# Two attention layers on one core: where the layer values, the last turn and the first weighted block stand in a hand-written order

## The chip, the cores and the metric

The kernel runs on one core of one Trainium2 chip. The metric is the device time of one execution in microseconds (us), the median over several executions. The hardware profiler records one execution more, with every instruction; durations in this text come from that record. Engines are named as in the profile: PE is TensorE (matrix products and turns), PEld its weight loads, DVE is VectorE, ACT is ScalarE, POOL is GpSimd, and SP is the engine that issues the transfers (DMA).

## The reference

The inputs are `x` (16 batches, 1024 nodes, 256 features, f32) and `adj` (16 x 1024 x 1024, int32, symmetric with ones on the diagonal). Every batch goes through two layers, each with a residual:

```python
# layer 0
h = relu(layernorm(x))
n = layernorm(h) * gamma1 + beta1                 # 8 heads of 32: q = k = v = n
a = softmax(where(adj > 0, n_q @ n_k.T / sqrt(32), -inf))
h = h + a @ n_k                                   # per head
x = x + h + gelu((layernorm(h) * gamma2 + beta2) @ W1 + b1) @ W2 + b2
# layer 1
f = relu(layernorm(x))
p = f @ W
l = (p @ a_1).T + p @ a_2 + (p @ a_12) @ p.T
t = softmax(where(adj > 0, leaky_relu(l, 0.2), -9e15))
x = x + elu(f @ W_1 + (t @ f) @ W_2)
```

The MLP is 256 to 1024 to 256. In the kernel the weights of layer 1 are folded beforehand: one matrix `wm` stands for `W a_12 W^T` in the logits, and `wo2` holds `W_2` with a further column `W a_1`, so that `gw = f @ wo2` gives the layer values `f @ W_2` and the term of `a_1` at once, and `(t @ f) @ W_2` becomes `t @ gw`.

## The kernel before, in words

**Two lanes of work.** All instructions of an engine run in the order in which the program lists them, and this order is planned by hand. The work is written as Python generators ("streams") that hand over after every piece, and each piece carries a place on a common scale; the stream with the smallest place goes on next. Two streams matter here. The attention of layer 0 for batch b+1 (`attention`) comes in units. The rest of batch b (`rest`: MLP, then layer 1) comes in pieces of 1.75 us planned width, or 0.9 for the short ones, and lies between those units. A piece that yields `True` moves the lane's place on. So one batch takes one repeat of about 210 us, and there are fourteen repeats with everything in them. The fifteenth MLP has no next prologue beside it, and the sixteenth has no attention beside it.

**Due times.** A planned clock advances with each piece and unit. `defer(t, f)` issues `f` when the clock has gone on by `t`; `run_deferred` issues what is due. So mask conversions, statistics, exponentials and transfers come into the order some pieces after the piece that asks for them. Other work waits as a turn: `ask(turn, c)` puts a turn of chunk `c` into a list, which `make_turns` works off between units; `wait_for(turn, c)` holds the lane until that has been done.

**The attention.** A batch has 8 key tiles of 128 and two halves of 512 queries. A unit computes the scores of four heads for one key tile (`s`, L994), VectorE adds the mask (L1007), ScalarE takes the exponential with its sums (L1014), and the product with the values follows a unit later (`o`, L1109). Because scores and mask are symmetric, one quarter of the exponentials isn't computed: while the first query half runs, `mirror` transposes blocks on VectorE (L1030), SP stores them to DRAM (`blocks`, L1037), and GpSimd adds them up (`part`, L1043) for the row sums, which SP stores as `rows` (L1058). For the second half `fetch(k)` loads them back as `em` (L1077), sixteen loads k = 0 to 15 per batch, eight for each of two head groups, and `weigh_mirrored(k)` multiplies them (`o`, L1091). `weigh_mirrored(k)` also defers `fetch(k + 2)` by 0.6: there are two buffers, so a load is issued only when the product two before it has used its buffer. In the second half a unit is followed by two such products. Three planned widths, which depend on the key tile, say how far the lane's place moves ahead of the first, between the two, and behind the second; what the other lane does in between follows from these (L1186):

```python
widths = ((0.8, 0.3, 0.05), (0.5, 0.45, 0.2), (0.4, 0.45, 0.3), (0.3, 0.5, 0.35))[kt - TPH]
yield widths[0]
weigh_mirrored(k)
yield widths[1]
weigh_mirrored(k + 1)
k += 2
yield widths[2]
```

SP also loads the int32 mask tiles (`adj`, L587), in halves that VectorE converts (L594); SP takes its instructions in order too.

**The rest of a batch.** Its 1024 rows are four chunks of two tiles. `expand(c)` is the first MLP product with its GELU (`ph`, `hid`), `contract(c, ..)` the second: per tile two pieces of four products into `po`, and then VectorE adds the residual into `xb` (L1327). `prepare1(c)` takes the statistics of a chunk and defers its normalized rows `ft` (L750, VectorE) by 5.0. `turn1(c)` transposes them on TensorE (`ptf`, L1349), and ScalarE writes them with a ReLU as `fT` (L1352). From `fT` come three things. `project_half(qh, oc)` gives `uT`, one output half `oc` for the query half `qh`, that is for two chunks (`puT`, L1364, copied by ScalarE, L1369). `values(t)` gives the layer values `gw` of one tile (`pg`, copied by VectorE for odd and by ScalarE for even tiles, L1379). `weights(c, i)` gives the logits of two key tiles `uT` for the queries of chunk `c` (`lg`); VectorE adds `gw`'s last column and the mask (L1397) and applies the leaky slope (L1402), ScalarE the exponential (L1403). Then `attend(t)` forms `own` (`pf`) and the product `pa` with the values, and stores the tile.

`ps_tile` gives every short product its PSUM tile from one pool of **three slots** (`ptf`, `po`, `puT`, `pg`, `lg`, `pa` and the turns of the next batch's prologue, `ptk`, among them): a product waits until the third product ahead of it has been read out. `with_values(pieces, c)` puts `values` of chunk `c` behind every second piece of a contraction, once `turn1(c)` has been made.

**The order around the change** is: `contract(2)` with the values of chunk 0 (tiles 0, 1), `contract(3)` with those of chunk 1 (tiles 2, 3), projection (0, 0), the last turn `turn1(3)`, projection (0, 1), values 4, logits 0, values 5, logits 1, projection (1, 0), values 6, projection (1, 1), values 7; then the remaining logits and `attend`.

Of the kernel before, what the change touches and what calls it, by code (L numbers as in the profile page):

```python
# [495 lines left out]
def fast_path(  # L496
# [29 lines left out]
    B, N, D = x.shape  # L526
# [9 lines left out]
    TPH = QW // P  # L536
# [25 lines left out]
    def ps_tile(shape, name, dtype=F32):  # L562
        return psm.tile(shape, dtype, tag="ps", name=name)
# [195 lines left out]
    def defer(us, f):  # L759
        deferred.append((clock[0] + us, len(deferred), f))  # L760

        return clock[0] + us
# [177 lines left out]
    def make_turns():  # L940
        room = 3 - open_sums[0] if open_sums[0] else 100
        while turns and turns[0][0] <= room:
            n, f = turns.pop(0)
            room -= n
            f()
# [22 lines left out]
    def attention(b, st):  # L968
# [96 lines left out]
        def gather(g):  # L1065
            r = blocks["sums", g] = denp.tile([P, NT // 2 * GH, TPH * GH], F32, tag="sums", bufs=1, name=f"gather_{b}_{g}")
            for a in range(GH):
                nc.sync.dma_start(
                    r[a * HD : (a + 1) * HD],
                    blocks["rows", g].rearrange("k (a i) e -> i (k a) e", i=HD)[:, :, a * TPH * GH : (a + 1) * TPH * GH],  # L1070
                )

        def fetch(k):
            g, t, half = k // (2 * TPH), k // 2 % TPH, k % 2
            if k == 0:
                blocks["e"] = midp.tile([P, 2, 2 * GH, P], F32, tag="mid0", name=f"em_{b}")
            nc.sync.dma_start(  # L1077
                blocks["e"][:, half],
                blocks[g][half * 2 * GH : (half + 1) * 2 * GH, t * GH : (t + 1) * GH].rearrange(
                    "k b i e -> (b i) k e"  # L1080
                ),
            )

        def weigh_mirrored(k):
            g, t, half = k // (2 * TPH), k // 2 % TPH, k % 2
            e = blocks["e"][:, half]
            if t == half == 0:
                acc[g, 1] = pso.tile([P, QW], F32, tag="o", name=f"o_{b}_{g}_1")
            o = acc[g, 1]
            for j in range(GH):  # L1090
                nc.tensor.matmul(  # L1091
                    o[j * HD : (j + 1) * HD, half * CW : (half + 1) * CW],
                    va[:, t, (g * GH + j) * HD : (g * GH + j + 1) * HD],
                    e[:, :, j * HD : (j + 1) * HD],
                    start=t == half == 0,
                    stop=False,
                )
            clock[0] += 0.45
            if k + 2 < 2 * TPH * NG:
                defer(0.6, lambda: fetch(k + 2))  # L1100
# [21 lines left out]
        def close(qh, g):  # L1122
            turns.append((1, lambda: finish(b, qh, g, *rl[g, qh], os[g, qh])))

        def invert(qh, g):
            r = smallp.tile([P, TPH, GH], F32, tag="rl", name=f"rl_{b}_{g}_{qh}")

            def f():
                if mirrored and qh == 0:
                    nc.vector.tensor_reduce(  # L1130
                        sums[0, g][:, :, :, 1].rearrange("p h t -> p t h"),
                        blocks["sums", g].rearrange("p k (t h) -> p t h k", h=GH),
                        axis=mybir.AxisListType.X,
                        op=ALU.add,
                    )
                nc.vector.tensor_reduce(
                    r.rearrange("p t j -> p j t"), sums[qh, g], axis=mybir.AxisListType.X, op=ALU.add
                )
                nc.vector.reciprocal(r, r)

            rl[g, qh] = r, defer(2.5 if mirrored and qh == 0 else 2.5, f)
# [8 lines left out]
        for n, u in enumerate(units):  # L1150
            qh, g, kt = u
            make_turns()
            es, rest_of_weights = scores(*u)
            go_on()
            rest_of_weights()
            first = n == 0 or units[n - 1][:2] != u[:2]
            last = n == len(units) - 1 or units[n + 1][:2] != u[:2]
            scored.append((weigh, (*u, es, first, last)))
            if not mirrored:
                if qh == NQH - 1 and kt % TPH == TPH - 1:  # L1160
                    invert(kt // TPH, g)
                    if kt < NT - 1:
                        close(kt // TPH, g)
                yield 1.0
                continue
            if qh == 0:
                if kt >= TPH:
                    mirror(g, kt, es)
                if n == NG * NT - 1:
                    defer(2.0, lambda: fetch(0))  # L1170
                    defer(2.2, lambda: fetch(1))
                if n == NT + 1:
                    gather(0)
                if n == NT + 3:
                    invert(0, 0)
                    close(0, 0)
                yield 1.0
                continue
            if n == NG * NT + 1:
                gather(1)  # L1180
            if n == NG * NT + 3:
                invert(0, 1)
                close(0, 1)
            if last:
                invert(1, g)
            widths = ((0.8, 0.3, 0.05), (0.5, 0.45, 0.2), (0.4, 0.45, 0.3), (0.3, 0.5, 0.35))[kt - TPH]  # L1186
            yield widths[0]
            weigh_mirrored(k)
            yield widths[1]
# [4 lines that stand above are left out]
    def go_on():  # L1194
        if scored:
            f, args = scored.pop()
            f(*args)
        clock[0] += 2.0
# [33 lines left out]
    def rest(b, st, tails):  # L1232
# [18 lines left out]
        def ask(turn, c):  # L1251

            def f():
                clock[0] += 0.5
                turn(c)
                turned.add((turn, c))
            turns.append((1, f))
            if not quarters[0]:
                make_turns()
# [49 lines left out]
        def contract(c, hid):  # L1309
            hid, ready = hid  # L1310
            run_deferred(ready)
            for i in range(TPC):
                t = c * TPC + i
                po = ps_tile([P, D], f"po_{b}_{t}")
                for f in range(FC):
                    matmul(
                        po,
                        hid[:, f, i * P : (i + 1) * P],
                        w2[:, f, :],
                        start=(f == 0),  # L1320
                        stop=(f == FC - 1),
                    )
                    if f == FC // 2 - 1:
                        open_sums[0] = 1
                        yield 1.75, True
                        open_sums[0] = 0
                nc.vector.tensor_add(xt[t], po, xt[t])  # L1327
                yield 1.75, True
# [128 lines left out]
        def with_values(pieces, c):  # L1457
            for i, piece in enumerate(pieces):
                yield piece
                if i % 2 == 1:  # L1460
                    yield from wait_for(turn1, c)
                    values(c * TPC + i // 2, st["fT"])
                    yield 0.9, i // 2 == 1
# [5 lines left out]
        hid = {0: (yield from expand(0))}  # L1469
# [16 lines left out]
        prepare1(1)  # L1486
        fT = st["fT"] = midp.tile([P, DC, N], F32, tag="mid1", name=f"fT_{b}")
        ask(turn1, 0)
        yield from with_values(contract(2, hid[2]), 0)
        prepare1(2)  # L1490
        ask(turn1, 1)
        yield from with_values(contract(3, hid[3]), 1)
        uT = midp.tile([P, DC, N], F32, tag="mid2", name=f"uT_{b}")
        prepare1(3)
        ask(turn1, 2)
# [1 line left out]
        def some_values(*ts):  # L1497
            for t in ts:
                values(t, fT)
                yield 0.9, t % 2 == 1  # L1500
# [5 lines left out]
        def some_weights(c, *pairs):  # L1506
            for i in pairs:
                first.append(weights(c, i))
                yield 1.75, True
# [2 lines left out]
        yield from wait_for(turn1, 0)  # L1512
        yield from wait_for(turn1, 1)
        yield from project_half(0, 0)
        if b < B - 1:
            ask(turn1, 3)
        yield from project_half(0, 1)
        if b == B - 1:
            ask(turn1, 3)
        yield from wait_for(turn1, 2)  # L1520
        yield from some_values(4)
        yield from some_weights(0, 0)
        yield from some_values(5)
        yield from some_weights(0, 1)
        yield from wait_for(turn1, 3)
        yield from project_half(1, 0)
        yield from some_values(6)
        yield from project_half(1, 1)
        yield from some_values(7)

        before = None
        for c in range(NCH):
# [186 lines left out]
```

## Time and profile before

| what | value |
|---|---|
| median of 3 runs | 3445.18 us (3441.09 to 3447.68) |
| the profiled execution | 3447.03 us |
| its span, first to last instruction | 3445.2 us |
| busy PE / DVE / ACT / POOL | 3250.0 / 2669.7 / 1987.4 / 1856.5 us |
| mean granted TensorE clock | 0.988 of full speed |
| moved by DMA | 404.81 MB, mean 118 GB/s |

The profiled execution stands 1.85 us above the median, and 1.8 us of it lie around the span. Busy times are sums over an engine's instructions; where a line of the profile names a releaser ("<- DVE ft"), it says what ended the idle time before the instruction. In a timeline each line holds start, duration, engine, source line, operation, result and operands, with the wait in brackets. PE's share of 94% says that it is almost never idle; where it is idle or slow in a repeat, and what is late there, has to be read from the timeline of a repeat.

### The profile page before, as it was taken

How to read it: one execution, taken by the hardware profiler on the slowest of the kernel's cores; microseconds unless marked ns; L12 is line 12 of the kernel's file. 1: busy time of each engine (PE TensorE's matmuls, PEld its weight loads, DVE VectorE, ACT ScalarE, POOL GpSimd, SP SyncE). 2: the span in 40 equal slices, each digit the busy share in tenths (PEclk: the TensorE clock that was granted, in tenths of full speed). 3: DMA queues.
4: the chain of work that ended last, by engine and by line, in shares of the span. 5: the costliest groups of instructions: out<-in, count | busy, mean ns of one | idle time of the engine just before them, and what ended most of it. 6: DMA issues, size and time to landing. Idle time of an engine off the chain costs nothing. (4 is left out here: it accounts for less than half of the span.)

```text
span 3445.2 us, 114688 instructions
## 1 busy us (share of the span) xinstructions
PE 3250.0 (94%) x48866; PEld 1597.5 (46%) x48866; DVE 2669.7 (77%) x4889; ACT 1987.4 (58%) x4808; POOL 1856.5 (54%) x2006
## 2 busy tenths in 40 slices
PE   6899999999999999999999999999999999999998
PEld 2244444444444444444444444444444444444477
DVE  5678787887878778787887887878788787877744
ACT  6765755647456474655646556575564745646542
POOL 4664663645656465563656737466364565635230
PEclk9999999999999999999999999999999999999999
DMA  5255455464554544545454555545546455554510
GB/s 134 50 123 145 104 122 125 112 159 102 128 120 116 144 112 122 129 114 143 112 133 112 122 139 119 140 106 125 125 112 159 100 131 118 121 142 102 128 38 14
DMA packets 741159, 404.81 MB, mean 118 GB/s; under 512 B 173217, under 2 KB 699937, under 8 KB 740641
## 3 DMA queue, kind: packets, MB, share of 16 engines
q1 hardware_dynamic: 740352, 397.14, 47.7%
q8 instruction: 386, 6.32, 0.8%
q14 instruction: 133, 1.08, 0.1%
q10 hardware_dynamic: 288, 0.26, 0.0%
HBM read 233.97 MB, written 146.54 MB: 110 GB/s over the span
## 5 line engine op out<-in xcount | busy, mean ns | idle before, releaser
L1014 ACT ACTIVATE e<-e 128x512 f32<-128x512 f32 x1504 | 929.3, 619 | 829.5 <-DVE e L1007 827.4
L1007 DVE TENSOR_TENSOR e<-s,mk 128x1024 f32<-128x1024 f32 x752 | 885.9, 1218 | 219.2 <-PE s L994 212.4
L574 PE MATMUL ph<-yT,w 128*32 128x256 f32 x7808 | 445.7, 379 | 23.5 <-DVE yT L1279 15.9
L574 PE MATMUL lg<-fT,uT 128*32 128x256 f32 x7680 | 455.7, 381 | 0.0
L994 PE MATMUL s<-kT 32*64 32x512 f32 x6272 | 451.3, 627 | 1.2 <-DVE e L1007 1.2
L574 PE MATMUL pa<-gw,e 128*32 128x258 f32 x7584 | 446.4, 380 | 0.1
L574 PE MATMUL po<-w,hid 128*32 128x256 f32 x7680 | 442.6, 379 | 0.0
L1109 PE MATMUL o<-e,va 128*32 128x512 f32 x3136 | 432.8, 619 | 1.4 <-ACT e L1014 1.4
L574 PEld LDWEIGHTS ph<-yT,w 128*32 128x32 f32 x7808 | 250.6, 110 | 226.8 <-DVE yT L1279 32.3
L574 PEld LDWEIGHTS po<-w,hid 128*32 128x32 f32 x7680 | 249.9, 110 | 203.0 <-issue 48.8
L574 PEld LDWEIGHTS lg<-fT,uT 128*32 128x32 f32 x7680 | 249.2, 110 | 195.3 <-issue 22.5
L574 PEld LDWEIGHTS pa<-gw,e 128*32 128x32 f32 x7584 | 247.5, 110 | 185.3 <-issue 26.2
L966 POOL TENSOR_TENSOR h<-h,ot 128x512 f32<-128x512 f32 x64 | 84.4, 1319 | 455.7 <-DVE ot L962 455.7
L1030 DVE STREAM_TRANSPOSE x<-e 128x1024 f32<-128x1024 f32 x240 | 296.2, 1239 | 42.3 <-ACT e L1014 40.8
L1043 POOL TENSOR_TENSOR part<-part,x 128x512 f32<-128x512 f32 x240 | 316.7, 1320 | 18.8
L1397 DVE SCALAR_TENSOR_TENSOR e<-lg,gw,mk 128x256 f32<-128x256 f32 x512 | 223.0, 476 | 112.0 <-PE lg L574 100.7
L1014 ACT ACTIVATION_READ_ACCUMULATOR e<-e 128x1 f32 x1504 | 281.5, 187 | 0.0
L1403 ACT ACTIVATE e<-e,shift 128x512 f32<-128x512 f32 x256 | 183.1, 716 | 158.4 <-DVE e L1402 150.5
L1303 ACT ACTIVATE hid<-ph,b1c 128x256 f32<-128x256 f32 x512 | 202.8, 466 | 83.4 <-PE ph L574 63.9
L1043 POOL TENSOR_TENSOR part<-x 128x512 f32<-128x512 f32 x120 | 155.4, 1295 | 176.2 <-DVE x L1030 114.7
L919 POOL TENSOR_TENSOR odd<-mk,mq 128x512 bf16<-128x512 fp8e5 x192 | 234.0, 1226 | 18.1 <-DVE uneven L926 15.6
L746 POOL TENSOR_TENSOR rs_c<-ve_c,mhalf 128x2 f32<-128x2 f32 x64 | 45.6, 713 | 359.4 <-DVE ve_c L744 323.9
(144 smaller groups left out, 4613.7 us busy)
## 6 DMA issues: line engine op xcount, KB each, us to landing
blocks<-x SPq DMA_DIRECT2D x480, 256.0 KB, 4.7
em<-blocks SPq DMA_DIRECT2D x240, 512.0 KB, 5.0
adj<-in_adj_dram SPq DMA_DIRECT2D x248, 256.0 KB, 3.9
h<-in_x_dram SPq DMA_DIRECT2D x64, 256.0 KB, 4.1
xb<-in_x_dram SPq DMA_DIRECT2D x128, 128.0 KB, 3.3
out_dram<-z SPq DMA_DIRECT2D x128, 128.0 KB, 3.9
rows<-row SPq DMA_DIRECT2D x120, 32.0 KB, 2.3
gather<-rows SPq DMA_DIRECT2D x120, 32.0 KB, 3.4
```

Of the source, the lines that this page charges most:

```text
L574: nc.tensor.matmul(out[c : c + HD], lhsT[:, c : c + HD], rhs, start=start, stop=stop)
L919: nc.gpsimd.tensor_tensor(odd.rearrange("p (u v x) -> p u v x", u=2, v=2), key.rearrange("p (u v x) -> p u v x", u=2, v=2), query.rearrang ...
L966: nc.gpsimd.tensor_add(ho, ho, ot.rearrange("p t j d -> p t (j d)"))
L994: nc.tensor.matmul(sc[j // 2][c : c + P // 2, j % 2, :], kT[r, g, kt * P + c : kt * P + c + P // 2], kT[r, g, qs], start=j >= by_pe, stop= ...
L1007: nc.vector.tensor_tensor(e, masked, mb, op=ALU.add)
L1014: nc.scalar.activation(e[:, j], masked[:, j], AF.Exp, scale=SCALE, accum_out=sums[kt // TPH, g][:, n, kt % TPH, qh : qh + 1],)
L1030: nc.vector.transpose(x[:, :, 2 * i : 2 * i + 2, :].rearrange("p c h j -> p h c j"), es[i].rearrange("p h (c i) -> p h c i", i=HD),)
L1043: add = lambda out, p, q: nc.gpsimd.tensor_tensor(out, p, q, op=ALU.add)
L1109: nc.tensor.matmul(o[j * HD : (j + 1) * HD, :], va[:, kt, (g * GH + j) * HD : (g * GH + j + 1) * HD], es[j // 2][:, j % 2, :], start=first ...
L1303: nc.scalar.activation(hid[:, f0 + i, :], ph[:, i, :], AF.Identity, bias=b1c[:, f0 + i : f0 + i + 1])
L1397: nc.vector.scalar_tensor_tensor(e[:, j, :], lg[:, j, :], gw[:, kt, D : D + 1], st[c // 2][:, kt // 2, qs, kt % 2], op0=ALU.add, op1=ALU.add,)
L1403: ready = defer(2.5, lambda: nc.scalar.activation(e, e, AF.Exp, bias=shift))
```

## The change

Two places change. In `attention` the three widths of the first of four key tiles of the second query half change, so that the first mirrored product stands further from its unit, and the second closer to the first. In `rest` the order of the pieces changes: the values of chunk 0 move from `contract(2)` to `contract(3)`; those of chunk 1 (tiles 2 and 3) stand behind the two first projections; the last turn is asked for behind the first logits piece, so behind two projections, two values and one logits piece; values 5 to 7 stand between and behind the two last projections. No instruction is added or removed.

```diff
@@ attention
-            widths = ((0.8, 0.3, 0.05), (0.5, 0.45, 0.2), (0.4, 0.45, 0.3), (0.3, 0.5, 0.35))[kt - TPH]
+            widths = ((0.95, 0.2, 0.0), (0.5, 0.45, 0.2), (0.4, 0.45, 0.3), (0.3, 0.5, 0.35))[kt - TPH]
@@ rest
         ask(turn1, 0)
-        yield from with_values(contract(2, hid[2]), 0)
+        yield from contract(2, hid[2])
         prepare1(2)
         ask(turn1, 1)
-        yield from with_values(contract(3, hid[3]), 1)
+        yield from with_values(contract(3, hid[3]), 0)
...
         yield from wait_for(turn1, 0)
         yield from wait_for(turn1, 1)
         yield from project_half(0, 0)
-        if b < B - 1:
-            ask(turn1, 3)
+        yield from some_values(2)
         yield from project_half(0, 1)
-        if b == B - 1:
-            ask(turn1, 3)
+        yield from some_values(3)
+        yield from some_weights(0, 0)
+        ask(turn1, 3)
+        yield from some_weights(0, 1)
         yield from wait_for(turn1, 2)
         yield from some_values(4)
-        yield from some_weights(0, 0)
-        yield from some_values(5)
-        yield from some_weights(0, 1)
         yield from wait_for(turn1, 3)
         yield from project_half(1, 0)
-        yield from some_values(6)
+        yield from some_values(5)
         yield from project_half(1, 1)
-        yield from some_values(7)
+        yield from some_values(6, 7)
```

## The prediction

> **What bounds the kernel now.** I read the page's first line, then the waits of TensorE alone, then the timeline of one of the fourteen repeats in which the MLP of a batch lies beside the attention of the next, the one that starts at 2113.3 us.
>
> ```profile
> PE 3250.0 (94%) x48866; PEld 1597.5 (46%) x48866; DVE 2669.7 (77%) x4889; ACT 1987.4 (58%) x4808; POOL 1856.5 (54%) x2006
> ```
>
> TensorE is busy 94% of the span, so its idle time (172 us of gaps in all) and its slow time are what an edit of the order can win. Columns below: who waited, for whom, us in total, times, longest.
>
> ```profile
> PE ptf L1349 <- DVE ft L750: 44.7, 15, 3.5
> PE o L1091 <- DMA em<-blocks: 25.1, 21, 3.1
> PE puT L574 <- DVE xb L1327: 19.6, 14, 1.9
> ...
> PE pg L574 <- ACT fT L1352: 9.4, 15, 0.9
> ```
>
> The first and third lie in one place, once per repeat (start, us, row):
>
> ```profile
> 2139.03 1.92 PE L574 MATMUL puT<-fT,wm 128*32 128x512 f32 x16 [1.43 <-DVE xb L1327]
> 2140.89 0.66 PE L1349 MATMUL ptf<-ident,ft 128*128 128x128 f32 x4
> 2144.65 0.67 PE L1349 MATMUL ptf<-ident,ft 128*128 128x128 f32 x4 [3.11 <-DVE ft L750]
> 2145.25 1.80 PE L994 MATMUL s<-kT 32*64 32x512 f32 x16
> 2146.99 1.94 PE L1109 MATMUL o<-e,va 128*32 128x512 f32 x8
> ```
>
> The last chunk's turn `ptf_3` waits 3.11 us for its input, and after that scores take 1.80 instead of 1.11 and the next product 1.94 instead of 1.07: the clock is halved. From `ptf_0` (2113.29) to the third logits piece `lg_0_2` (2164.36) this repeat takes 51.07 us; the fourteen take 49.4 to 52.8, mean 51.5, and differ mostly by this slow time (0 to 2.9 us, mean near 2). Now the same stretch as busy times (us; PE, PEld, DVE, ACT, POOL):
>
> ```profile
> 2129.60:2149.70 20.10, 15.57 (x176) 5.70 (x172) 17.02 (x37) 7.28 (x20) 16.11 (x18) 0.92 0.56 131
> ...
> 2113.30:2164.40 51.10, 45.51 (x624) 19.28 (x624) 44.77 (x90) 27.79 (x65) 32.91 (x37) 0.97 0.47 112
> ```
>
> VectorE has 44.8 us of work in the stretch, as much as TensorE's 45.5. From 2113.9 to 2144.8 it stands still for 1.1 us only. It is the second bound, and TensorE's waits are its lag.
>
> [...] 1.80 for 1.11 after 3.1 us, and in two of the fourteen repeats no slow time after the same wait. [...] Here a mask conversion pair (L594) takes 0.72 alone and more while GpSimd adds `part`:
>
> ```profile
> 2127.80 1.85 DVE L594 TENSOR_SCALAR mq<-adj 128x512 fp8e5<-128x512 int32 x2
> 2129.91 1.83 DVE L750 TENSOR_SCALAR ft<-xb,mv_d,rs_d 128x256 f32<-128x256 f32 x2
> ```
>
> **Part 1: the layer values and the last turn.** No instruction is added or removed; products, copies and turns change places. In the program's order `ptf_3` moves from right behind `ptf_2` to behind a unit of scores, `pg_3`, two logits pieces and `pg_4`. So the 3.11 us wait, the slow time (about 2), the 1.43 (slot of `po_7`), the 0.60 of `pg_0` on `fT` and the 0.46 of `ptk` can all go: 7.5 us. What is late next is VectorE. I add up its new order from `ft_1` (released by GpSimd at 1.5 us behind the anchor, 2114.73) to the mask step of the second logits piece, with start-to-start times of the timeline without collisions: four score pairs L1007 at 2.27, six statistics groups at 1.27, four stream transposes at 1.17, four conversion pairs at 0.65, three `ft` pairs at 0.70, three `xb` adds at 0.34, two `gw` copies at 0.33, sums and `ot` 1.80, two `nm` 0.27, two logits mask steps at 1.56: 9.08 + 7.62 + 4.68 + 2.60 + 2.10 + 1.02 + 0.66 + 1.80 + 0.27 + 3.12 = 32.95. Walking TensorE's order beside it, no product comes late enough to let VectorE rest, while TensorE waits about 1 us each at `puT_1_0` (slot held until `gw` of `pg_1` is copied), `pg_3` (ScalarE is behind `nm_2`), `pg_4` (slot, `gw` of `pg_3`), `ptf_3` (slot, mask step of `lg_0_0`) and `puT_0_1` (`fT_3` behind the second logits' exponential). Behind that last wait come 0.72 + 0.60 on ScalarE with hand-offs, 1.4, and then two `puT` at 1.72, three `pg` at 0.87, `ptk` 0.56, a unit of 1.04 + 0.88: 8.55. The stretch becomes 1.5 + 32.95 + 1.4 + 8.55 = 44.4 plus the collisions C with GpSimd.
>
> C is the unknown. In this repeat it was 3.2 up to `ft_3` (1.13 + 1.10 in the rows above, 0.56 in a later conversion, a 0.40 gap). In the new order `ft_3` follows a score pair, as the two rows above do, and so it and the conversion behind it fall into the additions of `part_1_6`; before, `ft_3` (2144.10) was just ahead of them (2145.02). That is 1.1 and up to 1.7 more. Ends: 3.2 and 6.0; I take 4.6. The stretch is then 49.0, against 51.5: 2.5 us won per repeat, 14 x 2.5 = 35 us (15 to 55 at the ends).
>
> The fifteenth MLP has no next prologue and waits 1.0 us at its turn: 1 us won. The last has no attention beside it and no wait; its new order keeps four products ahead of `ptf_3`, which cover the 1.9 us that `ft_3` needs there: nothing. If that cover were short, below 1 us once.
>
> **Part 2: the widths.** For the second head group the first mirrored product of `em` moves behind one more logits piece (1.73 us). The load that it sets free, the third of that group (k=10), is issued by SP, and in the new order stands behind both halves of the next mask tile's load, which wait for VectorE's conversion of the tile before. SP before:
>
> ```profile
> 2215.49 0.38 SPq L1077 DMA_DIRECT2D em<-blocks  x1
> 2219.98 0.81 SPq L587 DMA_DIRECT2D adj<-in_adj_dram  x2
> 2220.89 2.79 SPq L1077 DMA_DIRECT2D em<-blocks  x2
> ```
>
> So k=10 loses its early issue (2215.49) and takes the place of k=11 (2220.89), which is 1.2 us earlier now: the conversion no longer stands behind `en_3` and `z_3` (0.8), and the logits ahead of it end 0.43 earlier. Issue near 2219.7. A load there, behind the two mask halves, landed after 4.8 to 6.8 us (k=11) and 4.1 to 7.0 (k=14, the same place one mask tile pair later); I take 5.7: 2225.4. Its product stands at 2222.62 in both orders (the moves ahead of it add up to nothing). **TensorE waits 2.8 us** where it waited 0; behind it `pa_4` (3.5 us) and the chain follow. k=11 is issued 0.4 later and lands under `pa_4`, so its waits of 0.25 on average go. The other loads keep their distances. Is the clock halved by such a wait? Three `em` waits of 2.3 us and more are in the trace: after two (2.34 and 2.39) the logits behind took some 1.6 us longer, after the third (3.09) not. I take 0.6 x 1.65 = 1.0. Loss per repeat 2.8 - 0.25 + 1.0 = 3.55, x 14 = 50 us. Ends: landing 4.1 and no slow time, 1.2 - 0.25 = 0.95 (13 us); landing 7.0 and always slow, 4.1 - 0.25 + 1.65 = 5.5 (77 us).
>
> Other moves: the `rows` store of one tile now waits on SP behind a mask load from the second repeat on; it is gathered 30 us later, so this costs nothing. The `blocks` store behind it is not needed sooner than before.
>
> **Sum.** -35 - 1 + 50 = +14. The profiled execution took 3447.0 us (span 3445.2 and 1.8 around it), 1.9 above the median of the three runs. 3447.0 + 14 = 3461, as a median 3459.
>
> **Rivals.**
> - *Part 2 is cheap, faster.* One mechanism: k=10 lands 4.5 us after its issue and the wait of 1.6 us leaves the clock alone. Loss 14 x 1.35 = 19 against 36 won: 3428. It decides below 2.5 us of loss per repeat, a landing near 5.2 without slow time. For it: the page's median landing of `em` is 5.0. Against: the loads in just this place averaged 5.6 and 5.8.
> - *The two cancel.* C near 3.5 with 50 us lost, or a loss of 2.5: 3440 to 3452.
> - *VectorE gives nothing back.* C = 6.5, as when every conversion and `ft` pair of the stretch meets an addition: 50.9 us, 0.6 x 14 = 8 won, 3486. For it: two conversions in a row lost 2.3 us at 441.67. Against: GpSimd is idle for a third of the stretch.
> - *It doesn't do what it says:* the turn still waits long for `ft_3`. In my walk `ft_3` is done 1 to 2 us ahead of the slot; only the name of the wait would change. This is inside the C case.
>
> **Chances.** Forecast 0.42, VectorE gives nothing back 0.18 (both slower), cancel 0.15, cheap part 2 0.25. About 0.2%, 7 us, is what a measurement can tell from no change. Slower 0.60, same 0.15, faster 0.25. The range 3425 to 3489 leaves a tenth at each side; the slower cases' own is 3452 to 3489.
>
> **What would show it.** Right: the waits list has no `ptf <- DVE ft` of 3 us and no half clock behind it, but waits of about 1 us of `puT`, `pg` and `ptf` on VectorE and ScalarE; the stretch near 49 us; one new wait of some 2.8 us per repeat of `o L1091` on `em`, total rising from 25 towards 60 us. Wrong: the stretch at 47.5 or below (C overrated), or an `em` total that stays near 30.

## The result, and the profile after

The changed kernel takes 3459.39 us (median of 5 runs, 3458.43 to 3466.75) against 3447.15 us before (5 runs, 3441.09 to 3450.47). The ratio on record is 1.0046, 95% interval 1.0033 to 1.0059. It is not the quotient of the medians (1.0036), nor are the ratios below; by the medians the change is slower by 12.2 us. The execution that was profiled took 3466.75 us (span 3464.9), the longest of the five; the traces therefore differ by 19.7 us, the medians by 12.2, and counts taken from the trace of the change show a little more loss than its median.

The page after, its first line, and the waits of TensorE (who waited, for whom, us in total, times, longest):

```profile
PE 3257.5 (94%) x48866; PEld 1599.8 (46%) x48866; DVE 2664.0 (77%) x4889; ACT 1996.7 (58%) x4808; POOL 1854.1 (54%) x2006
```

```profile
PE o L1091 <- DMA em<-blocks: 56.7, 32, 3.7
PE puT L574 <- DVE gw L1379: 33.7, 14, 2.6
...
PE puT L574 <- ACT fT L1352: 14.7, 12, 1.2
PE ptf L1349 <- DVE e L1397: 13.8, 15, 0.9
PE pg L574 <- DVE gw L1379: 11.5, 8, 1.7
```

The 44.7 us of `ptf <- DVE ft` are gone from the list, and with them the 19.6 of `puT <- DVE xb`. In their place stand four rows that sum to 74 us, three of them on PSUM slots that VectorE empties late. The wait for `em` has risen from 25.1 to 56.7. The timeline of the repeat that starts at 2126.5 shows both places (start, us, row, wait in brackets):

```profile
2149.90 3.42 PE L574 MATMUL puT<-fT,wm 128*32 128x512 f32 x16 [2.45 <-DVE gw L1379]
...
2162.21 0.63 PE L1349 MATMUL ptf<-ident,ft 128*128 128x128 f32 x4 [0.94 <-DVE e L1397]
...
2166.11 1.92 PE L574 MATMUL puT<-fT,wm 128*32 128x512 f32 x16 [1.24 <-ACT fT L1352]
...
2225.83 1.05 PE L1091 MATMUL o<-em,va 128*32 128x256 f32 x16
...
2234.29 0.64 PE L1091 MATMUL o<-em,va 128*32 128x256 f32 x8 [2.19 <-DMA em<-blocks]
2234.74 5.35 PE L574 MATMUL pa<-gw,e 128*32 128x258 f32 x64
```

The projection behind the 2.45 us takes 3.42 where others take 1.90, and the product behind the 2.19 us takes 5.35 where it takes 3.67 in other places. Both ran partly at half clock: the clock records of the trace grant half (0.50) from 2149.54 and from 2234.87, for 3.41 us each. SP's timeline there says why `em` is late:

```profile
2215.65 0.36 SPq L1077 DMA_DIRECT2D em<-blocks  x1
2216.06 1.05 SPq L587 DMA_DIRECT2D adj<-in_adj_dram  x2
2218.95 0.34 SPq L1454 DMA_DIRECT2D out_dram<-z  x1
2228.05 0.81 SPq L587 DMA_DIRECT2D adj<-in_adj_dram  x2
2228.96 6.38 SPq L1077 DMA_DIRECT2D em<-blocks  x3
```

The load k=10 is issued at 2228.96 (the row holds k=10, 11 and 12), behind the two mask halves of 2228.05. Its buffer had been free since the product of k=8, which ran from 2225.83 (that row holds both k=8 and k=9). The mask halves were held up by VectorE, which reads the tile before them out of their buffers in a conversion that starts at 2227.61:

```profile
2227.61 0.76 DVE L594 TENSOR_SCALAR mq<-adj 128x512 fp8e5<-128x512 int32 x2
```

To see which part of a repeat changed, I laid the fourteen repeats of both traces side by side at fixed products (means in us):

| from, to | before | after | difference |
|---|---|---|---|
| `ptf_0` to `lg_0_2` | 51.40 | 48.53 | -2.87 |
| first MLP product behind the mirrored products (`ph`) to the next `ptf_0` | 75.19 | 76.99 | +1.79 |
| `lg_0_2` to the first mirrored product (k=0) | 12.90 | 11.86 | -1.04 |
| k=7 to k=8, and k=8 to k=9 | 9.14, 2.16 | 10.86, 0.43 | +1.73, -1.73 |
| k=9 to k=10 | 5.65 | 8.45 | +2.80 |
| k=10 to k=11 | 4.26 | 5.22 | +0.96 |
| the rest | 50.0 | 49.6 | -0.4 |
| a whole repeat | 210.7 | 211.9 | +1.25 |

The second row needs care. In the old order `ptf_0` came ahead of the last half of a `po` tile, because `contract(2)` had to wait for that turn before its first values; in the new one it comes behind it. So 1.79 us of work have left the first row's stretch through its front, and for the same work the stretch won 2.87 - 1.79 = 1.1.

### The profile page after: what moved, and what is told of

It reads as the page before. It is cut to its first block, busy times and chain, and to the rows that moved or that the text cites. A ratio compares the mean times of both kernels' runs of the same rounds, so it can differ in the third digit from the quotient of the medians.

```text
span 3464.9 us, 114706 instructions
## 1 busy us (share of the span) xinstructions
PE 3257.5 (94%) x48866; PEld 1599.8 (46%) x48866; DVE 2664.0 (77%) x4889; ACT 1996.7 (58%) x4808; POOL 1854.1 (54%) x2006
## 4 chain that ended last, share of the span: by engine, by line
PE 60%; DVE 21%; DMA 7%; POOL 5%; ACT 4%; issue 3%; SPq 0%; DVEq 0%; POOLq 0%; ACTq 0%
PE ph L574 10%; PE pa L574 10%; PE s L994 8%; PE lg L574 7%; PE po L574 6%; DVE e L1007 6%; PE o L1109 6%; DMA em<-blocks 5%; PE o L1091 2%; ACT e L1014 2%; POOL part L1043 2%; DVE e L1397 2%; PE pf L574 2%; PE puT L574 2%; DVE x L1030 2%
## 5 line engine op out<-in xcount | busy, mean ns | idle before, releaser
L574 PE MATMUL pa<-gw,e 128*32 128x258 f32 x7584 | 462.2, 390 | 0.0
L574 PE MATMUL po<-w,hid 128*32 128x256 f32 x7680 | 434.4, 379 | 0.0
L1109 PE MATMUL o<-e,va 128*32 128x512 f32 x3136 | 424.8, 609 | 1.4 <-ACT e L1014 1.4
L1043 POOL TENSOR_TENSOR part<-part,x 128x512 f32<-128x512 f32 x240 | 308.6, 1286 | 18.8
L746 POOL TENSOR_TENSOR rs_c<-ve_c,mhalf 128x2 f32<-128x2 f32 x64 | 45.6, 713 | 418.6 <-DVE ve_c L744 369.0
```

What stands on the lines that cost most here:

```text
L574: nc.tensor.matmul(out[c : c + HD], lhsT[:, c : c + HD], rhs, start=start, stop=stop)
L1043: add = lambda out, p, q: nc.gpsimd.tensor_tensor(out, p, q, op=ALU.add)
L1109: nc.tensor.matmul(o[j * HD : (j + 1) * HD, :], va[:, kt, (g * GH + j) * HD : (g * GH + j + 1) * HD], es[j // 2][:, j % 2, :], start=first ...
```

## The experiments

Each ran in four or five timed executions beside the kernel before (3447.0, 3447.4 and 3446.1 us in the three sets).

### The two parts apart

e1_order_only is the change without this line, and e2_widths_only is the kernel before with this line alone:

```diff
-            widths = ((0.8, 0.3, 0.05), (0.5, 0.45, 0.2), ...
+            widths = ((0.95, 0.2, 0.0), (0.5, 0.45, 0.2), ...
```

> The new order of values, turn and logits alone, with the widths of before. Theory A (as predicted: the order wins, the widths lose, and they add up): the trace of the changed kernel puts about 2.1 us per repeat to the order (the stretch with the piece that moved ahead of it 1.1, the first mirrored product 1.0), 14 x 2.1 = 30: about 3417 us, with the third load of the second head group on time. The prediction had 36 us. Theory B (the two parts need each other: the wait for the third load comes because TensorE is earlier after the new order): the wait of 2 us and more shows here too, and the time is within 10 us of before.

> The widths alone, with the order of before. Theory A: the third load of the second head group is issued behind the mask halves in every repeat, TensorE waits 2.4 to 2.8 us for it and the product behind it runs at half clock for about 1 us: 14 x 3.6 to 3.8 = 50 to 53, about 3499 us. Theory B (it is the earlier TensorE that makes the wait): under 20 us lost.

The order alone: **3415.15 us**, ratio 0.991 (0.9894 to 0.9925), 32 us faster. The widths alone: **3486.37 us**, ratio 1.0114 (1.0099 to 1.013), 39 us slower. Theory A's mechanism holds for both. In e1 the step from k=9 to k=10 is 5.65, as before; in e2 it is 8.51 with the old order around it, and TensorE's `em` total is that of the full change:

```profile
PE o L1091 <- DMA em<-blocks: 56.6, 32, 4.1
PE ptf L1349 <- DVE ft L750: 44.6, 15, 3.5
```

The change is in the main the sum of a gain and a loss from two different places (-32 + 39 = +7, measured +12). On top of the order, the widths cost 44 us (3459.4 - 3415.2). e2's loss was 11 us and more below its expectation. Most of that is the clock: the product behind the k=10 wait ran at half clock (5.5 to 5.6, once 6.8, instead of 3.94 from k=10 to k=11) in 3 repeats of 14, and in 10 of 14 in the full change, though the waits are equally long (2.7 and 2.6 us on average). Seven products at 1.69 us make 12 us between the two traces; the last section shows which of the change's products were slow; why there were fewer in e2 is not shown.

### The load of k=10 ahead of the mask halves

The full change, with the load of one mask tile deferred; TensorE, VectorE, ScalarE and GpSimd have exactly the order of the changed kernel:

```diff
-    def fetch_mask(b, t):
+    def fetch_mask(b, t, late=0):
...
-            nc.sync.dma_start(a, rows(adj, b, t, slice(c, c + QW)))
+            (lambda f: defer(late, f) if late else f())(lambda a=a, c=c: nc.sync.dma_start(a, rows(adj, b, t, slice(c, c + QW))))
...
-        raw = fetch_mask(b, ts[1])
+        raw = fetch_mask(b, ts[1], 1.0 if b and qh == 0 else 0)
```

> The full change, with one thing else: the load of the second mask tile of the next batch is deferred by one planned us, so that on SP's queue two of the loads of mirrored blocks (k=10, 11) stand ahead of its two halves. The order on all other engines is that of the changed kernel. Theory A (SP's order is what makes k=10 late): it is issued at its buffer's release, near 100 us behind the turn of the first chunk instead of 102.4, lands in about 4 us before its product at 105, the wait and the slow product go: 3459 - 53 = about 3406 us. Theory B (the later first product leaves too little time for any load, or the landing gets longer among the mask halves): a wait of over 1.5 us stays, 3435 or more.

**3413.79 us**, ratio 0.9904 (0.9889 to 0.9919), 8 us above theory A's figure: 45.6 us of the change's time vanish because one load and two mask halves change places on SP. SP in the same repeat, which here starts at 2088.8:

```profile
2188.77 0.38 SPq L1077 DMA_DIRECT2D em<-blocks  x1
2190.32 0.81 SPq L587 DMA_DIRECT2D adj<-in_adj_dram  x2
2191.22 4.01 SPq L1077 DMA_DIRECT2D em<-blocks  x2
```

One load, k=10, stands ahead of the halves (the expectation said two; k=11 stayed behind them). It lands 4.6 us after its issue, 0.8 ahead of its product, and k=9 to k=10 is 5.65 again. The mask halves are no later in the repeat than in the changed kernel, 101.5 us behind its start in both. So the widths cost their 44 us through SP's order, and with that mended they are worth nothing either: e1 and e3 agree within their intervals. (The deferral was not run without the widths, so a small effect of its own isn't excluded.)

### The last turn alone

The kernel before; only the request for the last turn moves:

```diff
         yield from project_half(0, 0)
-        if b < B - 1:
-            ask(turn1, 3)
         yield from project_half(0, 1)
-        if b == B - 1:
-            ask(turn1, 3)
         yield from wait_for(turn1, 2)
         yield from some_values(4)
         yield from some_weights(0, 0)
+        ask(turn1, 3)
         yield from some_values(5)
```

> The kernel before with only the last turn moved: it is asked for behind the first logits piece and lands behind the second; the values of all chunks and the projections keep their places, the widths too. Theory A (VectorE's lag bounds the stretch, the place of the values matters little): the 3.1 us wait and the half clock behind it go, a shorter wait on VectorE comes, and the gain is at least that of the whole new order: 2 to 4 us per repeat, 28 to 56 us, 3391 to 3419. Theory B (the values must be moved too, since projections and values fill the time that VectorE needs): under 1.5 us per repeat, 3426 or more.

**3426.82 us**, ratio 0.9936 (0.9923 to 0.995), 20 us faster: just inside theory B (3426 or more), so moving the values as well is worth some 12 us more. How the 20 us come about was a surprise. The page's first line and TensorE's waits:

```profile
PE 3228.1 (94%) x48866; PEld 1591.7 (46%) x48866; DVE 2695.4 (79%) x4889; ACT 1986.4 (58%) x4808; POOL 1855.8 (54%) x2006
```

```profile
PE ptk L824 <- ACT uT L1364: 17.4, 14, 1.3
PE lg L574 <- ACT gw L1379: 17.2, 14, 1.2
...
PE ptf L1349 <- DVE e L1397: 14.6, 14, 1.1
```

The 44.7 us of the turn have come back as three waits of at most 1.3 us, 42 us in all after taking off the 6.9 that `ptk` waited before; all gaps of TensorE behind its first product sum to 173 us, against 172. What fell is its *busy* time, from 3250.0 to 3228.1, while the mean granted clock rose from 0.988 to 0.996: here the turn's idle time, in three waits of at most 1.3 us in place of one of 3.1, came with less time at half clock.

### What GpSimd costs VectorE

Both kernels leave out two of GpSimd's wide additions (e5 from the kernel before, e6 from e3_full_em_first):

```diff
                 add(part, x[:, :, :, 0:8], x[:, :, :, 8:16])
-                add(part, part, x[:, :, :, 16:24])
-                add(part, part, x[:, :, :, 24:32])
                 add(part[:, :, :, :4], part[:, :, :, :4], part[:, :, :, 4:])
```

> The kernel before without the second and third of the wide additions of part on GpSimd (L1043, 128x512), so the row sums of the mirrored blocks are incomplete: some 2.6 us of GpSimd's work less per mirrored unit, nothing else changed. Theory A (VectorE's lag in the stretch comes to 3.4 us per repeat from rows that take longer beside GpSimd's additions): most of the excess of the conversions and of ft goes, the 3.1 us wait of the last turn falls to about 1 and the half clock behind it goes: 3 to 5 us per repeat, 42 to 70 us, 3377 to 3405. Theory B (VectorE is late for its own work, GpSimd doesn't matter): under 15 us, 3432 or more.

> The kernel of e3_full_em_first (3413.8 us) without the same two additions. Its VectorE rows have an excess of 5.3 us per repeat in the stretch, 3.2 to 3.6 of it at the two ft pairs. Theory A: ft falls to 0.7 a pair, the wait of projection (0, 1) on gw falls from 2.4 to under 1, with no half clock behind it (half of the repeats, 1.2 us): 2.7 to 3.7 us per repeat, 38 to 52 us, 3362 to 3376. Theory B: under 15 us, 3399 or more.

e5: **3408.21 us**, ratio 0.9891 (0.9874 to 0.9908), 39 us faster, just short of theory A's lower end, and not by the wait that I named. That wait did not move at all, and others went:

```profile
PE ptf L1347 <- DVE ft L750: 44.7, 15, 3.5
...
PE puT L574 <- DVE xb L1325: 3.8, 12, 0.3
```

(19.6 before; the 16.1 us of the first mirrored product on `os` have left the list. Together that is 32 of the 39 us.) So the 3.11 us are not made by collisions with these additions. VectorE's timeline of before shows what makes them, between the add that frees TensorE's slot and `ft_3`:

```profile
2138.57 0.41 DVE L1327 TENSOR_TENSOR xb<-po,xb 128x256 f32<-128x256 f32 x1
2138.90 1.23 DVE L1030 STREAM_TRANSPOSE x<-e 128x1024 f32<-128x1024 f32 x1
...
2144.02 0.17 DVE L744 TENSOR_SCALAR ve_a<-mv_a 128x2 f32<-128x2 f32 x1
2144.10 0.73 DVE L750 TENSOR_SCALAR ft<-xb,mv_d,rs_d 128x256 f32<-128x256 f32 x2
```

`xb` lets TensorE go at 2138.98, and VectorE works on without a gap until the first half of `ft_3` is there near 2144.5, 5.5 us later; TensorE has only a projection (1.85 to the next start) and `ptf_2` (0.6) to do meanwhile, and 5.5 - 2.45 is the wait to within 0.1. When VectorE gets to `xb` earlier, both ends move together, and the 3.11 stays. It is a matter of order, and the order is what the change mends.

e6: **3356.08 us**, 57.7 less than e3 (3413.79), more than expected; its stretch from `ptf_0` to `lg_0_2` is 45.15 instead of 48.70, and the wait of the projection on `gw` fell from 2.4 to 1.25. TensorE's wait in e6 (it was 33.7 us in the full change, and 35.7 in e3):

```profile
PE puT L574 <- DVE gw L1377: 16.9, 14, 1.3
```

The `ft` pairs of chunks 2 and 3 take 1.02 and 1.35 us in e6, so it is the additions that lengthen them. In the new order the additions show in the time more than in the old one. How much of the 58 us comes from VectorE's shorter rows, and how much from GpSimd being free sooner, was not tried apart. VectorE after, in the repeat shown above:

```profile
2139.02 2.45 DVE L750 TENSOR_SCALAR ft<-xb,mv_d,rs_d 128x256 f32<-128x256 f32 x2
...
2148.22 1.28 DVE L594 TENSOR_SCALAR mq<-adj 128x512 fp8e5<-128x512 int32 x2
2149.43 0.41 DVE L1379 COPY gw<-pg 128x257 f32<-128x257 f32 x1
...
2157.26 2.54 DVE L750 TENSOR_SCALAR ft<-xb,mv_d,rs_d 128x256 f32<-128x256 f32 x2
```

`ft_2` and `ft_3` take 2.45 and 2.54 where the pair ahead of the additions takes 0.73, and the copy of `gw` that TensorE waits for at 2149.9 comes behind the first of them and two slow conversions.

### Three ways around VectorE

e7 copies the values of tiles 1 and 3 on ScalarE (on top of e3):

```diff
-        (nc.vector.tensor_copy if t % 2 else nc.scalar.copy)(gw[:, t, : D + 1], pg[:, : D + 1])
+        (nc.vector.tensor_copy if t in (5, 7) else nc.scalar.copy)(gw[:, t, : D + 1], pg[:, : D + 1])
```

> The kernel of e3_full_em_first with the copies of the layer values of tiles 1 and 3 on ScalarE instead of VectorE; all else as there. Theory A (the wait of projection (0, 1) is a PSUM slot that stays full because the copy stands on VectorE behind two mask steps, statistics and conversions): ScalarE copies behind the exponentials of the unit, near 1.3 us earlier; the wait falls from 2.4 to about 1.1, the half clock behind it goes, the wait of 1.4 on the copy of tile 3 (half of the repeats) goes too: 20 to 38 us won, 3376 to 3394. Theory B (VectorE bounds the stretch whatever the slot does): only its two copies, 0.66 us per repeat, 9 us, 3405.

**3397.92 us**, ratio 0.9857 (0.984 to 0.9873): 15.9 below e3, more than VectorE's two copies and less than the slot's full price. It beats both kernels: 49 us below before, 61 below the change. TensorE's waits:

```profile
PE ptf L1349 <- DVE e L1397: 27.1, 15, 1.9
...
PE puT L574 <- ACT gw L1379: 17.4, 14, 1.8
```

The projection waits 1.20 in place of 2.45, as reckoned, but the last turn now waits 1.9 in place of 0.94: TensorE is earlier at VectorE's mask step, and VectorE is not.

e8 puts `ft` of chunks 2 and 3 on GpSimd instead (also on top of e3):

```diff
-                normalize(ft[c][:, i, :], xt[c * TPC + i], mv, rs, i)
+                normalize(ft[c][:, i, :], xt[c * TPC + i], mv, rs, i, nc.gpsimd if c >= 2 else nc.vector)
```

> The kernel of e3_full_em_first with the normalized rows ft of chunks 2 and 3 on GpSimd instead of VectorE. Theory A (these two pairs cost VectorE 2.45 us each where they meet an addition, and GpSimd has a third of the stretch free): VectorE wins up to 4.9 us per repeat, GpSimd makes a pair in 2.5 us behind its additions, the last turn waits little more than now: 14 to 45 us won, 3369 to 3400. Theory B (in order behind the additions of part GpSimd is late): the turns of chunks 2 and 3 wait 2 us and more for ft, and the half clock follows: slower than e3_full_em_first by 14 to 60 us, 3428 to 3474.

**3413.90 us**, the time of e3 (3413.79), and neither theory. The stretch won 2.5 us, and the next one, up to the first mirrored product, lost 2.2:

```profile
PE o L1091 <- ACT os L1118: 32.2, 14, 2.4
```

e9 is e7 with the values of tile 4 behind the last turn:

```diff
         yield from wait_for(turn1, 2)
+        yield from wait_for(turn1, 3)
         yield from some_values(4)
-        yield from wait_for(turn1, 3)
         yield from project_half(1, 0)
```

> The kernel of e7_copies_on_scalar (3397.9 us) with the values of tile 4 behind the last turn instead of ahead of it. In e7 the last turn waits 1.9 us for a PSUM slot that the first logits piece holds until VectorE has read it, and projection (1, 0) another 0.9 for fT, which ScalarE writes behind the second logits' exponential. Theory A (the slot and ScalarE's order, not VectorE's own work, make these waits): the turn takes the slot of tile 3's values, which is free early, ScalarE writes fT ahead of the second exponential, and projection (1, 0) starts about 1.5 us earlier: 1.0 to 1.5 us per repeat, 14 to 21 us, 3377 to 3384. Theory B (VectorE takes it back: its mask steps and the next scores set the pace): under 7 us, 3391 or more.

**3419.32 us**, ratio 0.9919 (0.9904 to 0.9933), 21 us slower than e7: a clear miss. The turn's wait fell as expected, from 1.9 to 0.5 on a slot and 0.5 on `ft`. But ScalarE's copy of tile 4 now stands behind a unit's exponentials, and projection (1, 1), which needs its slot, waits 2.14 in every repeat:

```profile
PE puT L574 <- ACT gw L1379: 49.4, 29, 2.1
```

## Why the prediction was right

The forecast case came true, 3459.4 against 3459, by a gain and a loss that were both there. That it came true to the microsecond is luck: by medians the gain was 32 us and not 36, and the loss 44 on top of the order (39 alone) and not 50, and the two errors nearly cancel.

- **Part 2, the loss.** The mechanism and the place hold, and in the trace of the change the size too: a landing of 5.7 us was assumed and 5.6 is the mean of the fourteen; a wait of 2.8 was reckoned, and k=9 to k=10 grew by 2.80. With the 0.96 from k=10 to k=11 that makes 3.76 per repeat, where 3.55 was reckoned; but this was the slowest of five executions, and the medians show 44 / 14 = 3.2 on top of the order and 39 / 14 = 2.8 alone. The half clock behind the wait, 0.6 times 1.65 in the sum, was 10 of 14 times 1.69 in the change and 3 of 14 in e2. The three waits that the factor came from could not show what it depends on. e2 and e3 show that SP's order is the cause.
- **Part 1, the gain.** Forecast 36 us, measured 32 in e1. Two terms of the sum were off and nearly cancelled. The stretch won 1.1 us per repeat, not 2.5. (The mean before is 51.40 and not 51.5, and the terms of 8.55 add up to 8.53; neither matters.) Here the step "from `ptf_0` ... this repeat takes 51.07" failed as a measure: `ptf_0` itself moves by a piece of 1.79 in the new order, and the sum took it for a fixed start. The 49.0 that was forecast for it and the 48.5 that was measured agree only because of that. C was about 5.3 (4.6 was taken, 3.2 before), and projection (0, 1), named `puT_1_0` there, waited 2.4 and not about 1, with half clock behind it in 6 of 14 repeats, which the sum had at nothing.
- **What was left out** is 1.04 us per repeat at the first mirrored product (k=0), whose wait of before has all but gone. The prediction had no term for anything behind `lg_0_2`. In e5, where GpSimd has less to do, the same wait goes without any change of order, and in e8, where GpSimd has more to do, it doubles (16.1 us to 32.2). That points to VectorE beside or behind GpSimd again, but which of the rows there decides was not tried apart. The line of before:

```profile
PE o L1091 <- ACT os L1118: 16.1, 14, 1.2
```

- **The waits named**: of the five, `ptf_3` (0.94) and the projection on `fT_3` (1.24; in the repeat shown the turn ended at 2162.84, and ScalarE copied it from 2165.49, behind the exponential of 2164.86) came as said, `pg_4` waited 1.4 in 8 repeats of 14 and `pg_3` once.
- **The rivals.** "Part 2 is cheap" needed a loss below 2.5 per repeat; it was 2.8 to 3.8, by the measure taken. "VectorE gives nothing back" needed C = 6.5, and "the two cancel" a time of at most 3452. The turn's long wait for `ft_3` is gone, so the change does what it says. The reading that TensorE's waits are VectorE's lag holds for the 3.11 us and for three of the four new rows; that collisions with the wide additions make the 3.11 us does not (e5).
- **The fifteenth repeat** was put at 1 us won. From its `ptf_0` to the next it went from 175.9 us to 175.7 in the change and 174.5 in e1, but its first marker moves by 1.8 and the next does not, so for the same work it grew by 1.6 and 0.4: no gain is to be seen there.

## What to carry to other kernels

Ask, for every product that an order moves back, which load it sets free, and read the *issuing queue's* order behind it: a load that lost its place ahead of two others cost more here than the whole reordering gained, and one deferred issue gave it back. Before comparing a stretch by a marker, check that the same work still lies between the markers. And run a change's parts apart even when the sum fits the forecast: a kernel 32 us faster was inside one that was 12 us slower.

## What the runs showed of the hardware

- **Which gaps were followed by half clock.** In e4 TensorE is idle as long as before (173 and 172 us) and the kernel is 20 us faster: gaps of at most 1.3 us have taken the place of 3.1 us gaps, and the mean granted clock is 0.996 in place of 0.988. The clock records of the traces of before and after show which gaps count. In each of the two, the stretches at half clock (17 and 24) start whole multiples of 3.413 us apart, to within 0.01 us, and last 3.41 or 6.83 us (the last, at the kernel's end, apart). With these points as the bounds of steps: between 200 and 3290 us, behind a step at full clock, the next step was at half clock in all 20 cases in which TensorE had been idle for over 2.2 us of the step, in none of 1728 under 1.8 us, and in 14 of 21 between. Behind a step that was itself at half clock, all 6 cases with over 0.6 us of idle time were followed by another, and none of 34 below. So waits of one length fared differently. Of the fourteen waits for `ft_3` before (3.1 to 3.5 us), half clock came behind the twelve that put 1.9 us of idle time or more into one step, and not behind the two that put at most 1.7 and 1.8 us into one. Of the fourteen waits for k=10 in the change, it came behind the ten with 2.08 us or more in one step (2.1 to 3.7 us long), and not behind the four with at most 1.73 (2.3 to 2.8 us long). There one step at half clock cost 1.69 us (5.63 - 3.94 from k=10 to k=11).
- **What GpSimd's additions cost.** An `ft` pair takes 0.73 us alone, and those of chunks 2 and 3 take 2.40 to 2.78 us beside them in the fourteen repeats of the changed kernel (1.02 and 1.35 in e6, without two of the additions). How an addition makes VectorE's rows longer was not shown. Without two of them per mirrored unit the kernel gained 39 us in the old order and 58 us in the new one.
